# Sums over keys by 32 by 32 block transposes and row sums on VectorE, in place of products with ones

## The chip, the cores and the metric

The kernel runs on one core of one Trainium2 chip. The metric is the device time of one execution, in microseconds, as the median of a few runs. A profiled execution gives, beside its time, the span of the core's work and a record of every instruction. The engines go by the names of the profile: PE is TensorE's matrix products and PEld its weight loads, DVE is VectorE, ACT is ScalarE, SP is the engine that issues all DMAs here.

## What is computed

Two layers run over a batch of 32 items with 512 rows of 512 numbers each. The change concerns the first layer, attention with 8 heads, weighted by an adjacency matrix:

```python
logits = jnp.einsum('bhqd,bhkd->bhqk', q, k) / np.sqrt(DK)
logits = logits + jnp.log(jnp.clip(adj, ADJ_MIN, None))[:, None, :, :]
attn = jax.nn.softmax(logits, axis=-1)
out = jnp.einsum('bhqk,bhkd->bhqd', attn, v)
...
return _layer_norm(x + out @ Wo.T + bo, gamma, beta)
```

The kernel forms exp(q k / 8) * max(adj, 1e-8) without a maximum taken off, multiplies by v, and divides afterwards by the sum over the keys. That sum is what the change computes in another way. The second layer is a graph attention with one logit per row and column; it is touched only where the order of its steps moves.

## The kernel before

**Layout.** Items are pipelined over three stages: while item b goes through its attention, item b-1 gets its output product, layer norm and the logits of layer 2, and item b-2 gets the products of layer 2. Steady items (b = 2 to 30 of 32) run as two functions, `first_two(b)` for heads 0 to 3 and `second_two(b)` for heads 4 to 7; two heads are a "pair" p, so `first_two` has pairs 0 and 1. Items 0 and 1 run through `slot`, item 31 through `joining_slot`, `slot` and `last_slot`. The order of the instructions on PE, DVE, ACT and SP is written out by hand: each engine takes its own in program order, and the only freedom is in waiting.

**Scores.** `score(b, p, kc, halved)` (L842) multiplies 128 keys with all 512 queries for both heads of a pair. The result goes to PSUM, either a two-bank tile of `ps_s` (two such tiles in turn, shared with the tiles `f` of `seven_qk`) or two of the three `lone` banks. ACT takes the exponential into a tile `at` of 128 keys by (2 heads, 512 queries); eight `at` tiles turn. `factor` (L887) multiplies by the adjacency on DVE.

**Sums over keys before.** `sums_in_place` (L900) adds the four `at` tiles of a pair on DVE, three additions of 128 by 1024. That leaves a sum over 128 partitions. `divide(b, p)` (L924) does it for two pairs at once on PE: four products with ones, each of 32 columns, into `lone[0]`. ACT copies the bank to R (L936), and two DMAs take the 4 by 512 sums to memory and back as a tile `c` of 128 by 16 (L939, L941). `divided(b, p)` (L944) checks their range, inverts them on DVE, stores them to memory and loads them spread out into R (L956, L959). `scale(b, p)` (L968) multiplies the attention output oT of the two pairs by R on DVE.

**Where these stand.** In `first_two(b)`: `divide(last, 2)`, eight scores, the layer-2 product `seven_z(b-2)` with its additions `extra[...]` and the block transposes of eP between, `both` (products of `at` with v), `sums_in_place` of pairs 0 and 1, `seven_wo` (output product of item b-1, with DVE additions L774 and L778 that free its banks), `seven_qk` of pairs 2 and 3. In `second_two(b)`: `divide(b, 0)`, eight scores, `seven_out(b-2)` (additions L795 and L801), `both`, `seven_qk` and `seven_v` of the next item, `divided(b, 0)`, `scale(b, 0)`. L670 to L672 are the three additions with which DVE ends a `seven_qk` and frees its `f` tiles for the next scores.

**SP's queue.** In this order: eP copies of item b-1, `divide(last, 2)`'s two, `divided(last, 2)`'s three, the loads of n and x, `divide(b, 0)`'s two, the loads of the next adjacency, `divided(b, 0)`'s three, the eP copies of the next item.

Of the kernel before, what the change touches and what calls it, by code (L numbers as in the profile page):

```python
# [9 lines left out]
FP = mybir.dt.float32  # L10
I32 = mybir.dt.int32
AF = mybir.ActivationFunctionType
ALU = mybir.AluOpType
AX = mybir.AxisListType
# [5 lines left out]
P = 128  # L20
# [5 lines left out]
BL = 32  # L26
# [4 lines left out]
def kernel(  # L31
# [55 lines left out]
    nc = tc.nc  # L87
    B, N, D = x.shape
    DK = D // HEADS
    NC = N // P  # L90
# [376 lines left out]
    def scaled(s, cs):  # L467
        nc.vector.tensor_mul(s["yb"][:, cs, :], s["n"][:, cs, :], over(K["gamma"], cs))
# [39 lines left out]
    def fast(ctx):  # L508
# [6 lines left out]
        dram = ctx.enter_context(tc.tile_pool(name="dram", bufs=2, space=bass.MemoryType.DRAM))  # L515

        S = [dict() for _ in range(B)]
        lone = [ps_l.tile([P, N], FP, name=f"m{i}") for i in "xyz"]

        class Turns:  # L520
# [363 lines left out]
        def factor(b, p, kc):  # L884

            at = S[b]["at", p, kc]
            nc.vector.scalar_tensor_tensor(  # L887
                at, cT[:, kc, :].unsqueeze(1).to_broadcast([P, 2, N]), ADJ_MIN, at,
                ALU.max, ALU.mult,
            )  # L890
# [4 lines left out]
        def sums_in_place(b, p):  # L895

            s = S[b]
            to = s["as", p] = s["at", p, 0]
            return [
                lambda kc=kc: nc.vector.tensor_add(to, to, s["at", p, kc]) for kc in range(1, NC)  # L900
            ]

        def values(b, p):
            s = S[b]
            s.setdefault("oT", [None] * NPAIR)

            def part(half):
                if half == 0:
                    s["po", p] = ps_o.tile([P, N], FP, tag="po", name=f"po_{b}_{p}")
                for kc in (2 * half, 2 * half + 1):  # L910
                    for j in range(2):
                        h = 2 * p + j
                        nc.tensor.matmul(  # L913
                            s["po", p][j * DK : (j + 1) * DK, :],
                            s["v"][h // 4][:, kc, ts(h % 4, DK)],
                            s["at", p, kc][:, j, :],
                            start=(kc == 0), stop=(kc == NC - 1),
                        )
                if half == 1:
                    s["oT"][p] = act.tile([P, N], FP, tag="oT", name=f"oT_{b}_{p}", bufs=6)  # L920
                    nc.scalar.copy(s["oT"][p], s["po", p])  # L921
            return [lambda: part(0), lambda: part(1)]

        def divide(b, p):  # L924


            s = S[b]
            ps = lone[0]
            for h in range(4):
                nc.tensor.matmul(  # L930
                    ps[h * BL : (h + 1) * BL, :], ones[:, :BL], s["as", p + h // 2][:, h % 2, :],
                    start=True, stop=True,
                )
            s["R", p] = act.tile([P, 2, N], FP, tag="R", name=f"R_{b}_{p}")
            r = s["R", p][:, 0, :]
            nc.scalar.copy(r, ps)  # L936
            m = 4 * N // P
            d0 = dram.tile([4, N], FP, tag="d0", name=f"d0_{b}_{p}")
            nc.sync.dma_start(out=d0, in_=r.rearrange("(h r) n -> h r n", r=BL)[:, 0, :])  # L939
            c = small.tile([P, 2, m], FP, tag="c", name=f"c_{b}_{p}")  # L940
            nc.sync.dma_start(out=c[:, 0, :], in_=d0.rearrange("h (a m) -> (h a) m", m=m))  # L941
            s["c", p] = c

        def divided(b, p):  # L944
            s = S[b]
            c = s["c", p]
            m = 4 * N // P
            i = 2 * b + p // 2
            nc.vector.tensor_scalar(c[:, 1, :], c[:, 0, :], SUM_MAX, None, ALU.is_le)
            nc.vector.scalar_tensor_tensor(  # L950
                c[:, 1, :], c[:, 0, :], SUM_MIN, c[:, 1, :], ALU.is_ge, ALU.mult,
                accum_out=seen[:, i : i + 1],
            )
            nc.vector.reciprocal(c[:, 0, :], c[:, 0, :])
            d1 = dram.tile([P, m], FP, tag="d1", name=f"d1_{b}_{p}")
            nc.sync.dma_start(out=d1, in_=c[:, 0, :])  # L956
            d1 = d1.rearrange("(k j a) m -> j k (a m)", k=2, j=2)
            for j in range(2):
                nc.sync.dma_start(  # L959
                    out=s["R", p][j * DK : (j + 1) * DK, :, :],  # L960
                    in_=d1[j].unsqueeze(0).to_broadcast([DK, 2, N]),
                )

        def scale(b, p):
            s = S[b]
            for k in range(2):
                oT = s["oT"][p + k]
                nc.vector.tensor_mul(oT, oT, s["R", p][:, k, :])  # L968

        def first_difference(b, to=None):  # L970

# [51 lines left out]
        def seven_z(b):  # L1023


            s = S[b]
            n, e = s["n"], s["eP"]
            s["zT"] = zT = L1
            s1 = third
            t1 = S[b + 1]["R", 2][:, 1, :].rearrange("p (c n) -> p c n", c=KH)  # L1030
            A = {f"{i + 1}{j + 1}": n[:, ts(j, KH), ts(i, H)] for i in range(2) for j in range(2)}
            E = {f"{i + 1}{j + 1}": e[:, ts(j, KH), ts(i, H)] for i in range(2) for j in range(2)}
            C = {f"{i + 1}{j + 1}": zT[:, ts(i, KH), ts(j, H)] for i in range(2) for j in range(2)}
            left = {1: A["11"], 2: A["12"], 3: A["12"], 4: A["22"], 5: s1, 6: A["11"], 7: A["21"]}
            right = {1: E["11"], 2: E["21"], 3: E["22"], 4: E["21"], 5: t1, 6: E["11"], 7: E["12"]}
            ps = {}
            sub = nc.vector.tensor_sub

            def mul(i, name, first=False):
                for m in range(KH):  # L1040
                    for t in range(KH):
                        halves(
                            ps[name][:, m, :].rearrange("p (c n) -> p c n", c=KH),
                            left[i][:, t, ts(m, P)], right[i][:, :, ts(t, P)],
                            first and m == 0 and t == 0, m == KH - 1 and t == KH - 1,
                        )

            def unit0():
                ps.update(zip("bac", long_banks(f"z{b}")()))
                mul(1, "a", True)  # L1050
                mul(5, "c", True)
                nc.scalar.copy(ps["b"], ps["a"])
                nc.scalar.copy(C["22"], ps["c"])

            def unit1():
                mul(6, "a")
                mul(2, "b")
                nc.scalar.copy(C["12"], ps["a"])
                nc.scalar.copy(C["11"], ps["b"])

            def unit2():
                mul(7, "a")
                mul(3, "c")

            def unit3():
                mul(4, "a")
                nc.scalar.copy(C["21"], ps["a"])

            def before0():
                nc.vector.tensor_add(s1, A["21"], A["22"])  # L1070

            def before1():
                sub(t1, E["12"], E["11"])
                sub(A["21"], A["11"], A["21"])

            def after0():
                sub(E["11"], E["22"], t1)
                sub(A["11"], s1, A["11"])

            def after1():  # L1080
                sub(E["12"], E["22"], E["12"])

            def before2():
                sub(A["12"], A["12"], A["11"])
                sub(E["21"], E["21"], E["11"])

            def after2():
                nc.vector.tensor_add(C["22"], ps["a"], C["22"])

            def after3():  # L1090
                nc.vector.tensor_add(C["12"], ps["c"], C["12"])
            return [unit0, unit1, unit2, unit3], [
                before0, before1, after0, after1, before2, after2, after3
            ]

# [200 lines left out]
        def run(units):  # L1296
            for u in units:
                u()
# [181 lines left out]
        def first_two(b):  # L1480
# [12 lines left out]
            zs, extra = seven_z(b - 2)  # L1493
            extra[0]()
            factor(b, 0, 0)
            factor(b, 0, 1)
            run(eT(b - 2))
            extra[1]()
            zs[0]()
            extra[2]()  # L1500
            extra[3]()
            scaled(S[b - 2], slice(KH, NC))
            turn_a((2, 3))
            zs[1]()
# [18 lines left out]
            next_qk = seven_qk(b, 2)  # L1523
            next_qk[0]()
            both(b, 1)
            run(sums_in_place(b, 0))
            scale(last, 2)
            first_sum(last)
            run(next_qk[1:4])
            run(sums_in_place(b, 1))  # L1530
            run(next_qk[4:])
            next_qk = seven_qk(b, 3)
            wos[1]()
# [3 lines left out]
            wo_adds[1][0]()  # L1537
            offset_rows(S[b - 2], slice(KH, NC))
            run(wo_adds[1][1:])
            wos[3]()  # L1540
            run(wo_adds[2])
            next_qk[0]()
            wos[4]()
            run(wo_adds[3])
# [38 lines left out]
        def second_two(b):  # L1583
# [1 line left out]


            last, nxt = b - 1, b + 1
            divide(b, 0)
            eight_scores(b, (2, 3))
            z_sums(b - 2)  # L1590
            ks, qs = dots_units(S[last], small, S[b]["R", 0][:, 1, :], last)
# [324 lines left out]
```

## Time and profile before

| what | value |
|---|---|
| median of three runs | 3345.13 us (3344.17 to 3346.44) |
| the profiled execution | 3345.6 us, of which the span is 3343.8 us |
| one steady item | 102.8 us |
| products with ones, L930 | 464 records, 605 ns each; four run side by side |
| ACT's copy of the sums, L936 | 63, 585 to 588 ns each |
| scaling with R, L968 | 126, 684 ns each |
| block transposes of 512 columns, L576 and L598 | 678 to 688 ns each |
| additions of 1024 columns, L900 | 348, 1218 ns each |

Instructions of DVE overlap a little at their ends, so a row of equal ones takes less than the sum of its durations: four transposes of 512 columns take 2.49 us. A matrix product in fp32 shows as two passes, and two products that fill different parts of the array show side by side; the duration of one says little, and the chain of waits says what a group of them costs. The TensorE clock was 1.0 in the whole run.

### The profile page before, as it was taken

The page shows a single profiled execution, that of the slowest core. Times are in us where ns is not written, and L with a number is a line of the kernel's source. Part 1 is how long each engine was busy: PE and PEld are TensorE (multiplying, and loading weights), DVE is VectorE, ACT ScalarE, POOL GpSimd, SP SyncE. Part 2 cuts the span into 40 slices and gives each one's busy share as a digit, 9 for nine tenths or more (in the row PEclk, how much of TensorE's full clock was granted, in tenths as well). Part 3 has the DMA queues.
Part 4 walks back from the last instruction along what each step waited for, and adds up shares of the span by engine and source line. Part 5 has one row for each costly group of instructions (what it writes and reads, how often), then busy time and mean ns, then how long its engine had stood idle before and what let it go on. Part 6 is the DMA issues. An engine that isn't in the chain of part 4 may idle for free.

```text
span 3343.8 us, 64256 instructions
## 1 busy us (share of the span) xinstructions
PE 3326.2 (99%) x25914; PEld 1929.8 (58%) x25914; DVE 3001.7 (90%) x5313; ACT 1407.5 (42%) x2559; POOL 0.9 (0%) x9
## 2 busy tenths in 40 slices
PE   9999999999999999999999999999999999999999
PEld 4555555565555555565555655556565656555545
DVE  7889898899988999889989889898899888998988
ACT  3444433434444344334443443444434434444343
POOL 0000000000000000000000000000000000000000
PEclk9999999999999999999999999999999999999999
DMA  5234242343433433334424234343343333442321
GB/s 127 45 75 93 61 85 66 68 93 67 87 69 60 89 83 71 74 58 86 93 61 85 62 71 93 67 87 69 58 92 83 71 74 58 86 93 61 84 71 48
DMA packets 881655, 252.84 MB, mean 76 GB/s; under 512 B 806732, under 2 KB 809036, under 8 KB 881352
## 3 DMA queue, kind: packets, MB, share of 16 engines
q1 hardware_dynamic: 881352, 248.67, 36.2%
q8 instruction: 206, 3.38, 0.4%
q14 instruction: 97, 0.79, 0.1%
HBM read 182.46 MB, written 34.65 MB: 65 GB/s over the span
## 4 chain that ended last, share of the span: by engine, by line
PE 97%; DVE 2%; ACT 1%; DMA 0%; issue 0%; SPq 0%; DVEq 0%; ACTq 0%
PE f L213 22%; PE mx L213 15%; PE my L213 15%; PE mz L213 15%; PE po L913 13%; PE sc L852 8%; PE my L852 2%; PE mx L852 2%; PE mz L852 2%; PE mx L930 1%; PE my L930 1%; PE mz L930 1%; PE mz L490 0%; PE my L326 0%; DVE at L869 0%
## 5 line engine op out<-in xcount | busy, mean ns | idle before, releaser
L887 DVE SCALAR_TENSOR_TENSOR at<-cT,at 128x1024 f32<-128x1024 f32 x468 | 551.7, 1216 | 0.0
L913 PE MATMUL po<-at,v 128*64 128x512 f32 x2048 | 467.6, 594 | 2.0 <-DVE fold_more L298 1.6
L900 DVE TENSOR_TENSOR at<-at,at 128x1024 f32<-128x1024 f32 x348 | 423.9, 1218 | 8.0
L861 ACT ACTIVATE at<-sc 128x1024 f32<-128x1024 f32 x328 | 332.9, 1075 | 53.4 <-PE sc L852 53.4
L852 PE MATMUL sc<-qT,kT 64*128 64x512 f32 x1312 | 317.3, 593 | 0.4 <-ACT at L861 0.4
L913 PEld LDWEIGHTS po<-at,v 128*64 128x64 f32 x2048 | 146.4, 137 | 247.4 <-issue 160.9
L921 ACT COPY oT<-po 128x512 f32<-128x512 f32 x128 | 74.9, 585 | 480.7 <-PE po L913 480.7
L213 PE MATMUL f<-xT,wq 128*64 128x256 f32 x2032 | 263.3, 379 | 0.0
L213 PE MATMUL f<-T,qk_s 128*64 128x256 f32 x2032 | 252.3, 379 | 0.1
L852 PEld LDWEIGHTS sc<-qT,kT 64*128 64x128 f32 x1312 | 120.2, 186 | 165.7 <-ACT at L861 79.8
L213 PEld LDWEIGHTS f<-xT,wq 128*64 128x64 f32 x2032 | 149.5, 137 | 97.1 <-issue 35.6
L213 PEld LDWEIGHTS f<-T,qk_s 128*64 128x64 f32 x2032 | 149.4, 137 | 82.6 <-issue 16.1
L655 ACT COPY f<-f 128x256 f32<-128x256 f32 x127 | 45.3, 357 | 345.4 <-PE f L213 345.4
L661 ACT ACTIVATE qT<-f,bq 128x256 f32<-128x256 f32 x127 | 60.1, 473 | 217.8 <-PE f L213 217.8
L852 PE MATMUL my<-qT,kT 64*128 64x512 f32 x254 | 133.5, 605 | 0.0
L213 PE MATMUL f<-xT,wk 128*64 128x256 f32 x1016 | 131.6, 379 | 0.0
L213 PE MATMUL f<-T,wk 128*64 128x256 f32 x1016 | 131.6, 379 | 0.0
L213 PE MATMUL f<-xT,qk_s 128*64 128x256 f32 x1016 | 131.6, 379 | 0.0
L852 PE MATMUL mz<-qT,kT 64*128 64x512 f32 x248 | 130.5, 606 | 0.0
L852 PE MATMUL mx<-qT,kT 64*128 64x512 f32 x234 | 123.2, 606 | 0.0
L213 PE MATMUL my<-eP,n 128*64 128x256 f32 x960 | 114.9, 380 | 2.2 <-DVE eP L576 1.7
L213 PE MATMUL mx<-eP,n 128*64 128x256 f32 x960 | 114.6, 380 | 0.5 <-DVE eP L576 0.5
(430 smaller groups left out, 6275.9 us busy)
## 6 DMA issues: line engine op xcount, KB each, us to landing
cT<-in_adj_dram SPq DMA_DIRECT2D x512, 64.0 KB
R<-d SPq DMA_DIRECT2D x126, 256.0 KB
x<-in_x_dram SPq DMA_DIRECT2D x124, 256.0 KB
n<-in_x_dram SPq DMA_DIRECT2D x31, 1024.0 KB
L<-in_adj_dram SPq DMA_DIRECT2D x60, 512.0 KB
eP<-L SPq DMA_DIRECT2D x480, 64.0 KB
out_dram<-yb SPq DMA_DIRECT2D x58, 512.0 KB
w<-dk SPq DMA_DIRECT2D x32, 256.0 KB
```

What stands on the lines that cost most here:

```text
L213: nc.tensor.matmul(to[ts(h, DK)], left[:, ts(h, DK)], right, start=start, stop=stop, skip_group_check=True,)
L655: nc.scalar.copy(ps["b"], ps["a"])
L661: nc.scalar.activation(q[:, H:], ps["a"], AF.Identity, bias=bq)
L852: nc.tensor.matmul(parts[j], s["kT", p][rows, ts(kc, P)], s["qT", p][rows, :], start=True, stop=True,)
L861: nc.scalar.activation(at, sc, AF.Exp, scale=SCALE)
L887: nc.vector.scalar_tensor_tensor(at, cT[:, kc, :].unsqueeze(1).to_broadcast([P, 2, N]), ADJ_MIN, at, ALU.max, ALU.mult,)
L900: lambda kc=kc: nc.vector.tensor_add(to, to, s["at", p, kc]) for kc in range(1, NC)
L913: nc.tensor.matmul(s["po", p][j * DK : (j + 1) * DK, :], s["v"][h // 4][:, kc, ts(h % 4, DK)], s["at", p, kc][:, j, :], start=(kc == 0), s ...
L921: nc.scalar.copy(s["oT"][p], s["po", p])
L930: nc.tensor.matmul(ps[h * BL : (h + 1) * BL, :], ones[:, :BL], s["as", p + h // 2][:, h % 2, :], start=True, stop=True,)
```

## The change

For pairs 0 and 1 of the steady items (`folded`, b = 2 to 30) the products with ones, ACT's copy and its two DMAs go. In their place `folded_sums(b)` returns, for each pair, the three additions of before (into the last `at` tile instead of the first) and two further DVE steps: the summed tile is transposed in place in blocks of 32 by 32, and a row sum over 32 elements reduces 128 by 1024 to 128 by 32. This adds 32 keys at a time, so four parts are left, one for each group of 32 partitions. `move_sums(b)` writes the 128 by 64 result to memory and reads it back with four DMAs in pieces of 16 numbers, so that the four parts of one query stand in one partition; `divided(b, 0)` adds them with one more small reduction. The inverted sums then stand in R in another order of queries (query 32 m + q at place 16 q + m), and `scale` reads R with a step of 16 numbers.

In the hand-written order the transposes and row sums stand in `first_two` between the groups of additions of `seven_wo`, with `move_sums` behind them. `second_two` only sets up the tile R where it called `divide(b, 0)`. Two other steps move: `A["21"]`'s subtraction goes from `before1` to `before0` of `seven_z`, ahead of the eP transposes (also in `joining_slot`, which shares it), and `factor(b, 0, 1)` goes from ahead of the eP transposes to behind `extra[3]`.

```diff
+        folded = {(b, 0) for b in range(2, B - 1)}
...
+        def folded_sums(b):
+            s = S[b]
+            s["ks"] = ks = small.tile([P, 4, 16], FP, tag="ks", name=f"ks_{b}", bufs=2)
+
+            def of(p):
+                to = s["at", p, NC - 1]
+                flat = to.rearrange("p j n -> p (j n)")
+                return [
+                    lambda kc=kc: nc.vector.tensor_add(to, to, s["at", p, kc])
+                    for kc in range(NC - 1)
+                ], [
+                    lambda: nc.vector.transpose(flat, flat),
+                    lambda: nc.vector.tensor_reduce(
+                        ks[:, 2 * p : 2 * p + 2, :].rearrange("p h m -> p (h m)"),
+                        flat.rearrange("p (a k) -> p a k", k=BL), AX.X, ALU.add,
+                    ),
+                ]
+            return of(0), of(1)
+
+        def move_sums(b):
+            s = S[b]
+            d0 = dram.tile([P, 64], FP, tag="d0", name=f"d0_{b}_0")
+            nc.sync.dma_start(out=d0, in_=s["ks"].rearrange("p h m -> p (h m)"))
+            c = small.tile([P, 4, 16], FP, tag="c4", name=f"c4_{b}", bufs=1)
+            for h in range(4):
+                nc.sync.dma_start(
+                    out=c[h * BL : (h + 1) * BL],
+                    in_=d0[:, h * 16 : (h + 1) * 16].rearrange("(k q) m -> q k m", q=BL),
+                )
+            s["c4"] = c
...
         def divided(b, p):
...
+            if (b, p) in folded:
+                c = small.tile([P, 2, m], FP, tag="c", name=f"c_{b}_{p}", bufs=2)
+                nc.vector.tensor_reduce(
+                    c[:, 0, :], s["c4"].rearrange("p k m -> p m k"), AX.X, ALU.add
+                )
+            else:
+                c = s["c", p]
...
         def scale(b, p):
             s = S[b]
             for k in range(2):
-                oT = s["oT"][p + k]
-                nc.vector.tensor_mul(oT, oT, s["R", p][:, k, :])
+                oT, r = s["oT"][p + k], s["R", p][:, k, :]
+                if (b, p) in folded:
+                    oT = oT.rearrange("p (m q) -> p m q", q=BL)
+                    r = r.rearrange("p (q m) -> p m q", q=BL)
+                nc.vector.tensor_mul(oT, oT, r)
...
             def before0():
                 nc.vector.tensor_add(s1, A["21"], A["22"])
+                sub(A["21"], A["11"], A["21"])
 
             def before1():
                 sub(t1, E["12"], E["11"])
-                sub(A["21"], A["11"], A["21"])
...
         def first_two(b):
...
             factor(b, 0, 0)
-            factor(b, 0, 1)
             run(eT(b - 2))
...
             extra[3]()
+            factor(b, 0, 1)
             scaled(S[b - 2], slice(KH, NC))
...
-            run(sums_in_place(b, 0))
+            sum0, sum1 = folded_sums(b)
+            run(sum0[0])
...
-            run(sums_in_place(b, 1))
+            run(sum1[0])
...
             run(wo_adds[1][1:])
+            run(sum0[1])
             wos[3]()
             run(wo_adds[2])
+            run(sum1[1])
+            move_sums(b)
...
         def second_two(b):
...
-            divide(b, 0)
+            S[b]["R", 0] = act.tile([P, 2, N], FP, tag="R", name=f"R_{b}_0")
```

More of the change, by code (lines that the diff above doesn't have):

```diff
@@ L939, in divide @@
             nc.sync.dma_start(out=d0, in_=r.rearrange("(h r) n -> h r n", r=BL)[:, 0, :])
-            c = small.tile([P, 2, m], FP, tag="c", name=f"c_{b}_{p}")
+            c = small.tile([P, 2, m], FP, tag="c", name=f"c_{b}_{p}", bufs=2)
             nc.sync.dma_start(out=c[:, 0, :], in_=d0.rearrange("h (a m) -> (h a) m", m=m))
@@ L945, in divided @@
             s = S[b]
-            c = s["c", p]
             m = 4 * N // P
             i = 2 * b + p // 2
+            if (b, p) in folded:
+                c = small.tile([P, 2, m], FP, tag="c", name=f"c_{b}_{p}", bufs=2)
+                nc.vector.tensor_reduce(
[3 more added lines that the diff above has]
+                c = s["c", p]
             nc.vector.tensor_scalar(c[:, 1, :], c[:, 0, :], SUM_MAX, None, ALU.is_le)
```

## The prediction

> **What bounds the kernel now.** I read the page first, then the chain of waits, then the busy time by stage over two halves of one steady item, and last the timelines of VectorE and TensorE around the two places that the change touches. The page and its chain:
>
> ```profile
> PE 3326.2 (99%) x25914; PEld 1929.8 (58%) x25914; DVE 3001.7 (90%) x5313; ACT 1407.5 (42%) x2559; POOL 0.9 (0%) x9
> ...
> PE 97%; DVE 2%; ACT 1%; DMA 0%; issue 0%; SPq 0%; DVEq 0%; ACTq 0%
> ```
>
> TensorE sets the time, and VectorE has 10% left. So a TensorE microsecond taken off is worth one only while VectorE is not late. By stage, from the start of one `divide` to the next:
>
> ```profile
> 1738.30:1789.66 51.36, 51.36 (x413) 29.55 (x416) 45.25 (x72) 18.26 (x32) 0.00 (x0) 1.00 0.35 61
> 1789.66:1841.13 51.47, 51.47 (x413) 29.49 (x416) 48.20 (x95) 25.58 (x48) 0.00 (x0) 1.00 0.39 88
> ```
>
> The columns are the stretch, its length, and the busy time of PE, PEld, DVE, ACT, POOL, then clock, DMA share and GB/s. VectorE is idle 6.11 us in the first half (`first_two`) but only 3.27 us in the second (`second_two`). What `divide(b, 0)` costs on the chain (start, us, what):
>
> ```profile
> 1785.35 4.32 PE f L213 x40
> 1789.66 1.00 PE mx L930 x8
> 1790.66 0.62 PE my L852
> ```
>
> Its four products run side by side: 1.00 us an item, not 4 x 0.6.
>
> Where VectorE waits before that point (start, us, instruction, idle before it):
>
> ```profile
> 1778.56 0.69 DVE L778 TENSOR_TENSOR n<-mx,n 128x512 f32<-128x512 f32 x1 [0.18 <-PE mx L213]
> 1779.16 0.68 DVE L778 TENSOR_TENSOR n<-mz,n 128x512 f32<-128x512 f32 x1
> 1780.21 0.69 DVE L778 TENSOR_TENSOR n<-my,n 128x512 f32<-128x512 f32 x1 [0.37 <-PE my L213]
> 1781.94 0.69 DVE L778 TENSOR_TENSOR n<-mx,n 128x512 f32<-128x512 f32 x1 [1.04 <-PE mx L213]
> 1785.39 0.69 DVE L778 TENSOR_TENSOR n<-mx,n 128x512 f32<-128x512 f32 x1 [2.76 <-PE mx L213]
> ...
> 1790.05 0.41 DVE L672 TENSOR_TENSOR kT<-f,kT 128x256 f32<-128x256 f32 x1
> ```
>
> Idle of 0.37 + 1.04 + 2.76 us is the cover for the new work. After it VectorE is packed until L672, and L672 frees the bank of the second score of `second_two`.
>
> The other place is the start of `first_two`:
>
> ```profile
> 1736.57 1.28 DVE L968 TENSOR_TENSOR oT<-oT,R 128x512 f32<-128x512 f32 x2
> ...
> 1737.77 1.30 DVE L598 STREAM_TRANSPOSE cT<-cT 128x512 f32<-128x512 f32 x2
> ...
> 1739.63 0.41 DVE L672 TENSOR_TENSOR kT<-f,kT 128x256 f32<-128x256 f32 x1
> ...
> 1740.19 1.88 PE L852 MATMUL sc<-qT,kT 64*128 64x512 f32 x8
> ```
>
> `scale(b, 0)` is the L968 pair. L672 ends at 1740.04 and the score that needs its bank starts at 1740.19. A handoff from VectorE to a waiting TensorE costs as much:
>
> ```profile
> 1438.65 0.69 DVE L1073 TENSOR_TENSOR R<-eP 128x512 f32<-128x512 f32 x1
> ...
> 1439.49 1.95 PE L213 MATMUL my<-R,third 128*64 128x256 f32 x16
> ```
>
> 1438.65 + 0.69 = 1439.34, so 0.15 us. At 1740 there is therefore no slack (0.03 us at most): whatever VectorE is late by in `second_two`, TensorE pays.
>
> **What the Trainium skill says.** "SBUF — State Buffer", section "Door 1: The DMA port swizzle", gives SBUF lines of 16 bytes, full rate only with two or more hits on a line, and a penalty where each access goes to a new one; "GPSIMD Engine Reference", section "Performance pitfalls for Q7 kernels", measures one cycle more an element (1.9 to 2.9) for steps over 8 bytes on GpSimd. No VectorE row of this trace has such a step with enough elements to show it. "VectorE: DVE Perf Modes", section "The perf-mode tier table", has `tensor_reduce` at one element a cycle; the trace has no large one. The same page, section "Walkthrough: the 8-slice pipeline in each mode", says of the plain 1x mode that it "makes no assumptions. fp32, weird strides, PSUM operands — all work"; the trace agrees on the rate for dense fp32 (1024 elements in 1.14 us), and is silent on steps.
>
> **Part by part, per item, for the 29 items b = 2 to 30.**
>
> Removed: four products, 1.00 us of TensorE; the first score pass costs 0.62 us after it against 0.42 for the next, and I leave that 0.2 where it is, since `slot` shows it after products of 64 columns too (1.92 against 1.72 for the first score at 119.85). ACT's copy (0.585 us) and two small DMAs are off the path.
>
> Added in `first_two`: two in-place transposes and two row sums, of 1024 elements a partition. The transpose is taken from L576: 2.49 us for four of 512, as fast as a tensor_tensor, so 1.14 for 1024 like L887 (4.62 for four):
>
> ```profile
> 1758.70 4.62 DVE L887 SCALAR_TENSOR_TENSOR at<-cT,at 128x1024 f32<-128x1024 f32 x4
> ...
> 1763.90 3.74 DVE L900 TENSOR_TENSOR at<-at,at 128x1024 f32<-128x1024 f32 x3
> ```
>
> L900, each reading its forerunner's output, steps by (3.74 - 1.22)/2 = 1.26. So a pair is 1.26 + 1.14 = 2.40, two are 4.80. Bounds for a row sum: 1.07 (1024 elements at the rate of L887's step) to twice 1.14.
>
> Placed from 1779.76: first pair to 1782.16, two L778 to 1783.36 (the second ends 1783.45; TensorE's last product of `seven_wo` wants its bank at 1783.45 in stream, stall about 0.12), second pair to 1785.76, against 1785.39 before. So L672 ends 0.37 later, 1790.83, and the second score starts 1790.98 (0.15 handoff). TensorE alone would be there at 1791.55 - 1.00 + 0.12 = 1790.67. VectorE ends last, and of 1.00 us only 1791.55 - 1790.98 = 0.57 is gained. The wait at L795 (1.72 idle before it) takes up 0.57 + 0.37, so nothing is carried from there into the rest of `second_two`.
>
> Added in `second_two`: the reduction over four parts, 64 elements to 16, about 0.24 (L949's 0.17, its 0.21 step to a dependent, a few more elements). Then `scale(b, 0)`: L968 now reads R at steps of 64 bytes. Bounds: no extra (step 0.60 each) and one cycle more an element, 512 / 0.96 GHz = 0.53 us each, 1.07 for both. Nothing excludes either; a gain is excluded. I take 1.07, since two pages price it and none says that VectorE is exempt. Behind it on VectorE stand L598, L670 and L672, and the second score waits for L672: 0.24 + 1.07 - 0.03 = 1.28 us of TensorE stall.
>
> Moved: L1074 ahead of the eP transposes (in `joining_slot` it leaves a chain that TensorE waits for: about 0.6 us once), and one L887 to behind L1081. The latter stands before L1084, which has 0.93 idle before it: 1.14 - 0.93 - cadence 0.09 leaves it 0.12 late, L1088 also, and the product that waits for L1088's bank about 0.10.
>
> Moved on SP: the small store and four gathers of 64-byte pieces are issued near 1786, after the loads of x (issued until 1772) and before anything at 1804; the result is needed at 1829.8. Some 6 us for five DMAs (the old pair took 1.7 us from issue to next issue) leave over 30 us. Without that cover each late microsecond would be one of VectorE's, then TensorE's. The d1 store, the R loads and the eP copies behind them on SP come 0.24 later, but TensorE is 1.28 later too.
>
> Sum: -0.57 + 1.28 + 0.10 = +0.81 us, times 29 = +23.5. Eight items lost 3.4 us to late eP copies (halves of 51.5 to 52.3 instead of 51.36); with TensorE later, most of that goes: -3.4. Joining item: -0.6. Together +19.5: the profiled execution's 3345.6 (span 3343.8 plus 1.8) becomes 3365; the median shown, 3345.13, lies 0.5 under it, so 3364.5. 3364.
>
> **The rivals.**
> (a) The strided read is free. Then +0.24 - 0.03 + 0.10 - 0.57 = -0.26, times 29 = -7.5, joining -0.6: 3337, faster. For it: the sentence on weird strides. Deciding point: 0.26 us for both multiplications, 0.13 each.
> (b) A part penalty, about a third more (0.2 each): +0.14 an item, 3348, no change.
> (c) Row sums at two cycles an element: 1.07 more for each of two, all of it at the second score: 2.14 x 29 = +62 on the forecast, 3426. Against it: the one-cycle price of the page.
> (d) VectorE is nowhere late: the whole 1.00, 29 us, 3316. Against it: the packed stretch to L672.
> (e) The gathers land late: needs 30 us more; under 1%.
>
> **How the numbers follow.** Forecast 0.58, (a) 0.28, (b) 0.08, (c) 0.03, (d) 0.03. About 0.2% (6.7 us) is what a measurement can tell from no change. Faster: most of (a), and (d): 0.26. Same: a part of (a), (b), a little of the forecast: 0.14. Slower: 0.60. The forecast's own range is 3355 to 3374 (row sums 0.15 longer each add 9). Signs are split, so the range takes (a) in: 3334 to 3374.
>
> **What would show it.** Right: L968 of pair 0 at 1.1 to 1.2 us instead of 0.68, L672 ending over 1 us later against `divide`, TensorE idle over 1 us before the second score of `first_two`, transposes of 1024 and row sums of 1.2 us each. Wrong: L968 unchanged (then a), or TensorE waiting before the second score of `second_two` for longer than 0.4 us (then c). No cover in the gathers would show as VectorE idle before its 64-element sum.

## The result, and the profile after

The changed kernel takes 3327.82 us (median of 6 runs, 3326.12 to 3329.62), the kernel before 3344.56 in the same comparison. The ratio is 0.9949, with an interval of 0.9936 to 0.9962. It is faster by 16.7 us, 0.5%. The forecast was 3364 us, slower by 19, with a range of 3334 to 3374: wrong in sign, and the time lies under the range.

The page of the changed kernel's profiled execution (3328.74 us, span 3327.0), busy times and the shares of the chain that ended last:

```profile
PE 3307.9 (99%) x25682; PEld 1892.2 (57%) x25682; DVE 3153.7 (95%) x5458; ACT 1393.4 (42%) x2530; POOL 0.9 (0%) x9
...
PE 65%; DVE 24%; DMA 5%; ACT 3%; issue 2%; SPq 2%; DVEq 0%; ACTq 0%
```

VectorE is busy 152 us longer and stands at 95%; TensorE is busy 18 us less. The chain now runs over VectorE for 24%. That number says little: a chain goes to whatever released an instruction last, even where the release cost nothing. TensorE is still busy 99% of the span, so what counts is where TensorE starts late.

The same two halves of a steady item in the changed kernel (columns as in the prediction; the cut between them is now the first score of `second_two`, since the product that marked it is gone):

```profile
1728.02:1779.79 51.77, 51.72 (x411) 29.40 (x409) 50.32 (x77) 18.36 (x32) 0.00 (x0) 1.00 0.34 62
1779.79:1830.25 50.46, 50.46 (x403) 29.26 (x401) 48.27 (x96) 24.99 (x47) 0.00 (x0) 1.00 0.40 90
```

Between the same points of the kernel before (its products start at 1738.23, the first score of `second_two` at 1790.59):

```profile
1738.23:1790.59 52.36, 52.36 (x419) 29.71 (x417) 46.25 (x75) 18.26 (x32) 0.00 (x0) 1.00 0.34 60
1790.59:1841.06 50.47, 50.47 (x404) 29.32 (x400) 47.20 (x92) 25.58 (x48) 0.00 (x0) 1.00 0.40 89
```

So the second half is unchanged, and the first gives 0.59 us: 1.00 of products removed, less 0.41 lost again. Times 29 items, 0.59 is 17.1 us; the spans differ by 16.8.

The new and the slower instructions, from the costliest groups of the changed kernel (line, engine, operation, tiles, count, then busy us, mean ns and idle before; L1013 is `scale`, L917 the transpose, L918 the row sum, L986 the sum of the four parts):

```profile
L1013 DVE TENSOR_TENSOR oT<-oT,R 128x512 f32<-128x512 f32 x126 | 100.7, 841 | 0.0
L917 DVE STREAM_TRANSPOSE at<-at 128x1024 f32<-128x1024 f32 x58 | 71.6, 1235 | 0.0
L918 DVE TENSOR_REDUCE ks<-at 128x32 f32<-128x1024 f32 x58 | 70.8, 1221 | 2.0
L986 DVE TENSOR_REDUCE c<-c 128x16 f32<-128x64 f32 x29 | 7.4, 254 | 0.0
```

L1013 mixes 68 dense and 58 strided ones; 841 ns is no instruction's duration. With 684 for the dense ones (L968 before), the strided ones are (126 x 0.841 - 68 x 0.684) / 58 = 1.03 us each. (The busy time of the group, 100.7, is less than 126 x 0.841, because neighbours overlap.)

**Where 0.32 of the 0.41 is lost: the start of `first_two`.** First the kernel before, its timeline there (start, us, instruction, idle before it; the rows of a view count passes up to its end, and four passes are one score; L930 is `divide(last, 2)`, L670 the first of the three additions; the last one, L672, ended at 1740.04):

```profile
1738.23 1.07 PE L930 MATMUL mx<-at,ones 128*32 128x512 f32 x8
1738.99 0.39 DVE L670 TENSOR_TENSOR qT<-f,qT 128x256 f32<-128x256 f32 x1
...
1739.76 0.19 PEld L852 LDWEIGHTS sc<-qT,kT 64*128 64x128 f32 x2 [0.23 <-issue]
...
1740.19 1.02 PE L852 MATMUL sc<-qT,kT 64*128 64x512 f32 x4
```

The weights of the second score load at 1739.76, before L672 ends. In the places below where this score does wait, its weights load only after the release (1730.19, 1846.21), so this speaks against a wait for L672, though the score starts 0.15 after its end; the experiments settle it. By them, L670 was the one that the score needed, and that was done at 1739.38. This line was there to be read before the prediction. Now the same place in the changed kernel (the same lines of the program stand one to 45 further down: L671 and L673 are the first and the last addition, L966 the products, L853 the score):

```profile
1726.65 1.97 DVE L1013 TENSOR_TENSOR oT<-oT,R 128x512 f32<-128x512 f32 x2
1728.02 1.06 PE L966 MATMUL mx<-at,ones 128*32 128x512 f32 x8
1728.54 1.29 DVE L599 STREAM_TRANSPOSE cT<-cT 128x512 f32<-128x512 f32 x2
1729.76 0.38 DVE L671 TENSOR_TENSOR qT<-f,qT 128x256 f32<-128x256 f32 x1
1730.19 0.30 PEld L853 LDWEIGHTS sc<-qT,kT 64*128 64x128 f32 x4 [0.88 <-DVE qT L671]
1730.20 1.13 PE L853 MATMUL sc<-qT,kT 64*128 64x512 f32 x4
1730.40 0.40 DVE L673 TENSOR_TENSOR kT<-f,kT 128x256 f32<-128x256 f32 x1
```

The weight load waits for L671, the first addition, and the score starts 0.06 after that ends, while the last addition, L673, runs until 1730.80. Counted from the products, the first addition ends at 1.15 us before (1739.38 - 1738.23) and at 2.12 after: 0.97 later, 0.69 of it the two strided multiplications (1.97 against 1.28 us), the rest the reduction. The score starts at 1.96 before and 2.18 after: 0.22 later. So the kernel before had 0.75 us of slack here, where the prediction had 0.03. The score then takes 0.10 more: its weights were not loaded ahead, and its first pass takes 0.53 us to the next one instead of 0.43. The fourth score starts at 1732.02, 4.00 us after the products, against 3.68 before. Together 0.32.

**The other end: `second_two`.** The packed stretch of VectorE before it, and the second score there (timeline of the changed kernel; L779 are `seven_wo`'s additions):

```profile
1769.85 1.24 DVE L917 STREAM_TRANSPOSE at<-at 128x1024 f32<-128x1024 f32 x1
...
1771.12 1.22 DVE L918 TENSOR_REDUCE ks<-at 128x32 f32<-128x1024 f32 x1
...
1772.26 0.68 DVE L779 TENSOR_TENSOR n<-my,n 128x512 f32<-128x512 f32 x1
...
1772.85 0.68 DVE L779 TENSOR_TENSOR n<-mx,n 128x512 f32<-128x512 f32 x1
...
1773.59 1.49 PEld L213 LDWEIGHTS mx<-wo_s,oT 128*64 128x64 f32 x16 [0.34 <-DVE n L779]
...
1779.72 0.39 DVE L671 TENSOR_TENSOR qT<-f,qT 128x256 f32<-128x256 f32 x1
...
1780.36 0.42 DVE L673 TENSOR_TENSOR kT<-f,kT 128x256 f32<-128x256 f32 x1
...
1780.75 1.45 PE L853 MATMUL sc<-qT,kT 64*128 64x512 f32 x6
```

The second score starts at 1780.75, before L673 ends at 1780.78, so it cannot have waited for it, and L671 had been done for 0.64 us. TensorE starts that score 0.96 after the first one at 1779.79, the same distance as in `first_two` before (1739.23 to 1740.19): no wait. The whole 1.00 us of the products is kept here, not 0.57. The remaining 0.10 of the loss is the weight load at 1773.59, which waits for an addition behind the first transpose and row sum, as forecast.

### The profile page after: what moved, and what is told of

Its sections match the earlier page's. It is cut to its first block, busy times and chain, and to the rows that moved or that the text cites. A ratio compares the mean times of both kernels' runs of the same rounds, so it can differ in the third digit from the quotient of the medians.

```text
span 3327.0 us, 64024 instructions
## 1 busy us (share of the span) xinstructions
PE 3307.9 (99%) x25682; PEld 1892.2 (57%) x25682; DVE 3153.7 (95%) x5458; ACT 1393.4 (42%) x2530; POOL 0.9 (0%) x9
## 4 chain that ended last, share of the span: by engine, by line
PE 65%; DVE 24%; DMA 5%; ACT 3%; issue 2%; SPq 2%; DVEq 0%; ACTq 0%
PE f L213 14%; PE mx L213 10%; PE mz L213 10%; PE my L213 10%; PE sc L853 8%; PE po L949 8%; DVE at L888 5%; DVE yb L802 4%; DVE R L392 3%; DMA out_dram<-yb 2%; DVE L L436 2%; DMA eP<-L 2%; DVE L L446 2%; ACT L L451 2%; PE my L853 2%
## 5 line engine op out<-in xcount | busy, mean ns | idle before, releaser
L853 PE MATMUL sc<-qT,kT 64*128 64x512 f32 x1312 | 319.8, 597 | 2.4 <-DVE qT L671 0.7
L853 PEld LDWEIGHTS sc<-qT,kT 64*128 64x128 f32 x1312 | 120.8, 185 | 174.4 <-ACT at L862 71.0
L853 PE MATMUL my<-qT,kT 64*128 64x512 f32 x254 | 133.5, 605 | 0.0
L853 PE MATMUL mz<-qT,kT 64*128 64x512 f32 x248 | 130.5, 606 | 0.0
L853 PE MATMUL mx<-qT,kT 64*128 64x512 f32 x234 | 123.2, 606 | 0.0
```

The source lines that it names most:

```text
L853: nc.tensor.matmul(parts[j], s["kT", p][rows, ts(kc, P)], s["qT", p][rows, :], start=True, stop=True,)
```

## The experiments

The question was which addition frees the second score's bank. Theory F: the first one, so the second score has slack and the removed products pay in full. Theory L, the prediction's own reading: the last one, with no slack. A third, M: the moved steps carry the gain. The kernel before took 3344.46 us (median) in the runs shared by the first four experiments and 3344.78 in those of the others.

**R read without a step.** The changed kernel, with `scale` reading R densely. The divisors then meet other queries, so the output is another one; the instructions are the same in number and size.

```diff
                 if (b, p) in folded:
-                    oT = oT.rearrange("p (m q) -> p m q", q=BL)
-                    r = r.rearrange("p (q m) -> p m q", q=BL)
+                    r = r
```

> The changed kernel, but scale reads R of pair 0 without a step, so the sums meet the wrong queries. Theory F (first addition): the bank of the second score of first_two is freed by the first addition of seven_qk (L671), which had about 0.7 us to spare in the kernel before and is 0.98 us late in the changed one; the stepped read is 0.69 us of that. Without it the lateness is 0.29 us, the stall of about 0.26 us an item goes, 29 x 0.26 = 7.5 us: near 3320 us. Theory L (last addition, no slack, as the prediction had it): every bit of lateness is paid, 0.69 x 29 = 20 us: near 3308 us. Theory M (the gain comes from the two moved steps): no change from 3328 us.

3319.59 us, ratio 0.9922 (0.9909 to 0.9936). That is 8.2 us under the changed kernel, as F has it; an item takes 101.92 us instead of 102.23, and 0.31 is the whole loss at the second score. Had the penalty been paid in full, it would have been 0.69 x 29 = 20 us.

**The transposes behind the additions.** The changed kernel, with the two transposes that stand between `scale` and the additions put behind them:

```diff
             scale(b, 0)
-            turn_a((0, 1))
             run(seven_qk(nxt, 1))
+            turn_a((0, 1))
```

> The changed kernel with the two transposes of turn_a((0, 1)) behind seven_qk(nxt, 1) in second_two, so that its three additions come 1.2 us earlier on VectorE. Theory F: the stall of 0.26 us an item before the second score of first_two goes, near 3320 us. Theory L: 0.98 us an item, 28 us, near 3300 us. Theory M: no change from 3328 us.

3319.87 us, ratio 0.9926 (0.9912 to 0.9939): F again. All work is still there. The additions come 1.2 us earlier, and again 0.31 us an item is gained and no more. Its timeline there (L966 are the products):

```profile
1724.90 1.07 PE L966 MATMUL mx<-at,ones 128*32 128x512 f32 x8
1725.41 0.43 DVE L671 TENSOR_TENSOR qT<-f,qT 128x256 f32<-128x256 f32 x1
...
1726.41 1.30 DVE L599 STREAM_TRANSPOSE cT<-cT 128x512 f32<-128x512 f32 x2
...
1726.86 1.88 PE L853 MATMUL sc<-qT,kT 64*128 64x512 f32 x8
```

The second score stands 1.96 us behind the products, as in the kernel before.

**A delay ahead of all three additions.** The kernel before, with three small additions on VectorE:

```diff
+        pad = const.tile([P, P], FP, name="pad")
+        nc.gpsimd.memset(pad, 1.0)
...
             turn_a((0, 1))
+            for _ in range(3):
+                nc.vector.tensor_add(pad, ones, ones)
             run(seven_qk(nxt, 1))
```

> The kernel before with three VectorE additions of 128 by 128 (0.2 us each, 0.6 us in all) ahead of seven_qk(nxt, 1) in second_two. Theory F: within the 0.7 us of slack, 0 to +3 us (3344.6 to 3348). Theory L: 0.57 us an item, +16.5 us, near 3361 us.

3351.36 us, ratio 1.0022 (1.0014 to 1.0029): 6.9 us slower, between the two. The dose was larger than thought:

```profile
1844.16 1.06 PE L932 MATMUL mz<-at,ones 128*32 128x512 f32 x8
1844.92 0.90 DVE L1650 TENSOR_TENSOR pad<-ones 128x128 f32<-128x128 f32 x3
...
1845.74 0.42 DVE L672 TENSOR_TENSOR qT<-f,qT 128x256 f32<-128x256 f32 x1
...
1846.21 0.30 PEld L854 LDWEIGHTS sc<-qT,kT 64*128 64x128 f32 x4 [0.76 <-DVE qT L672]
1846.22 1.99 PE L854 MATMUL sc<-qT,kT 64*128 64x512 f32 x8
```

The first addition (L672 in this kernel) ends 2.00 us after the products, 0.85 later than before. With the slack of 0.75 read above, the score should start 0.10 late. It does: 2.06 against 1.96. With another 0.10 for the weights not loaded ahead, 0.20 x 29 = 5.8 of the 6.9 us. L, at this dose, would have cost (0.85 - 0.03) x 29 = 24 us for the wait alone. So the run decides against L, but only with its trace: both forecasts, 0 to 3 us and 16.5 us, missed, since they were worked out from too small a dose.

**The same delay between the first addition and the other two.** The kernel before, where only theory L has the second score late:

```diff
...
-        def seven_qk(b, p):
+        def seven_qk(b, p, late=False):
...
                 nc.vector.tensor_add(q[:, H:], ps["c"], q[:, H:])
+                if late:
+                    for _ in range(3):
+                        nc.vector.tensor_add(pad, ones, ones)
                 nc.vector.tensor_add(k[:, H:], ps["a"], k[:, H:])
...
-            run(seven_qk(nxt, 1))
+            run(seven_qk(nxt, 1, True))
```

> The kernel before with the same 0.6 us of VectorE work between the first addition (q) and the two others (k) of that seven_qk. Theory F: the first addition is not moved and the third score's bank has 0.9 us to spare, 0 to +3 us. Theory L: the last addition is what counts, +16.5 us, near 3361 us.

3352.92 us, ratio 1.0023 (1.0014 to 1.0033). It is 8.5 us slower, and again both forecasts missed. The time alone does not separate the theories; the timeline does (L672 is the first addition here, L677 the last):

```profile
1845.57 1.06 PE L935 MATMUL mz<-at,ones 128*32 128x512 f32 x8
...
1846.34 0.38 DVE L672 TENSOR_TENSOR qT<-f,qT 128x256 f32<-128x256 f32 x1
...
1847.53 1.99 PE L857 MATMUL sc<-qT,kT 64*128 64x512 f32 x8
...
1847.82 0.41 DVE L677 TENSOR_TENSOR kT<-f,kT 128x256 f32<-128x256 f32 x1
...
1848.35 0.33 PEld L857 LDWEIGHTS sc<-qT,kT 64*128 64x128 f32 x4 [0.63 <-PE my L857]
```

The second score starts 1.96 us after the products, unmoved, 0.70 us before the last addition ends at 1848.23. This excludes L directly. The row of 8 passes holds two scores; the weights of the third load at 1848.35, just behind that end, and it is the third score that loses here: 0.07 us by the start of the next. So the two `ps_s` tiles come free one by one, the second score's by the first addition, the third's by the last. The other 0.15 us an item comes further down, most of it in `seven_z`, where TensorE's products start up to 0.17 later than before. What in it is late was not taken apart. The halves show 0.22 an item, 6.4 of the 8.5 us; some 2 more are single items that took longer than the others (5.3 us in all in this execution, 3.3 before). The prediction puts such items down to late eP copies; no run here tests that.

**The moved steps put back.** The changed kernel, with `A["21"]` and `factor(b, 0, 1)` where they stood before:

```diff
             factor(b, 0, 0)
+            factor(b, 0, 1)
             run(eT(b - 2))
...
             extra[3]()
-            factor(b, 0, 1)
             scaled(S[b - 2], slice(KH, NC))
...
             def before0():
                 nc.vector.tensor_add(s1, A["21"], A["22"])
-                sub(A["21"], A["11"], A["21"])
...
             def before1():
                 sub(t1, E["12"], E["11"])
+                sub(A["21"], A["11"], A["21"])
```

> The changed kernel with the two moved steps (A["21"] and factor(b, 0, 1)) put back where they were. Theory M: they carry the gain, near 3344 us. Theory F: the gain is the removed products' 1.00 us less the stalls; without the moves the eP transposes start 0.54 us later against the scores, which the 0.45 us to spare before the second product of seven_z doesn't cover, and the third product gets its operands some 0.3 us late: 0.1 to 0.35 us an item, 3331 to 3338 us.

3328.46 us, ratio 0.995 (0.9937 to 0.9964), the changed kernel's time within 0.6 us. M falls. What F had added for the moves, 0.1 to 0.35 us an item, was too much as well: they cost and bring nothing that can be measured.

**Transposes and row sums taken out.** In their place a copy of 32 columns for each pair, so that the last part of the sums over keys, over the 128 partitions, is left out:

```diff
-                    lambda: nc.vector.transpose(flat, flat),
-                    lambda: nc.vector.tensor_reduce(
+                    lambda: nc.vector.tensor_copy(
                         ks[:, 2 * p : 2 * p + 2, :].rearrange("p h m -> p (h m)"),
-                        flat.rearrange("p (a k) -> p a k", k=BL), AX.X, ALU.add,
+                        flat[:, :BL],
                     ),
```

> The changed kernel with the transposes and row sums left out: 32 columns of each summed tile are copied into ks instead, so the divisors are other numbers. Theory F: the two pairs stand in idle time of VectorE but for 0.10 us an item at the last product of seven_wo: 2.9 us, near 3325 us. The prediction's reading, in which they cost 0.43 us of the gain at the second score of second_two: 12.5 us, near 3315 us.

3323.96 us, ratio 0.9937 (0.9924 to 0.9951). Some 4.8 us of VectorE work an item is worth 3.9 us in all, 0.13 an item (the usual item takes 102.11 us instead of 102.23): the 0.10 at `seven_wo` and little else. Had the second score of `second_two` waited for VectorE, as the prediction had it, 0.43 an item would have come back.

**Both losses mended.** The changed kernel with the transposes behind the additions, and with both row sums behind the additions `wo_adds[2]` of `seven_wo`, for which its last product waits:

```diff
             run(wo_adds[1][1:])
-            run(sum0[1])
+            run(sum0[1][:1])
             wos[3]()
             run(wo_adds[2])
-            run(sum1[1])
+            run(sum1[1][:1])
+            run(sum0[1][1:])
+            run(sum1[1][1:])
             move_sums(b)
...
             scale(b, 0)
+            run(seven_qk(nxt, 1))
             turn_a((0, 1))
-            run(seven_qk(nxt, 1))
```

> The changed kernel with turn_a((0, 1)) behind seven_qk(nxt, 1), and the order of the new steps in first_two as transpose 0, wo_adds[2], transpose 1, sum 0, sum 1. Theory F: both stalls go (0.26 and 0.10 us an item): 3317 us, 3 us under the run with the late turn_a alone. If the second stall isn't that of the last product of seven_wo: 3320 us.

3316.55 us, ratio 0.9914 (0.99 to 0.9927), faster than both kernels, and 3.3 us under the run with the late transposes alone: 0.11 an item, the loss at `seven_wo`. Its first half:

```profile
1722.78:1774.14 51.36, 51.36 (x410) 29.48 (x408) 49.92 (x74) 18.27 (x32) 0.00 (x0) 1.00 0.36 63
```

51.36 is 52.36 - 1.00: the products' whole microsecond, with VectorE still at 49.92 of 51.36. 28.2 us under the kernel before is 0.97 x 29.

**What a step costs.** One execution of the changed kernel with multiplications of 128 by 512 put ahead of its work, the second operand read with a step of 1, 2, 4, 8 and 16 numbers, then the first operand, both, and the result with 16, and last the second operand with 32:

```diff
...
+        for _ in range(2):
+            nc.vector.tensor_mul(pad_o, pad, pad)
+            nc.vector.tensor_mul(pad_o.rearrange("p (m q) -> p m q", m=2), pad.rearrange("p (m q) -> p m q", m=2), pad.rearrange("p (q m) -> p m q", m=2))
...
```

> The changed kernel with products of 128 by 512 on VectorE added at its start, the second operand read with steps of 1, 2, 4, 8, 16 and 32 numbers, then the first operand, both operands and the result with a step of 16. From the changed kernel's L1013 (1.03 us against 0.68): step 16 near 1.03. If lines of 16 bytes count, step 2 as step 1, steps 4 to 32 alike, slower than step 1. If only both streams together count, a stepped first operand costs as the second, and both more.

The timeline of VectorE there, in that order:

```profile
3.28 0.69 DVE L1796 TENSOR_TENSOR L<-L 128x512 f32<-128x512 f32 x1 [3.28 <-POOL L L1793]
4.01 0.69 DVE L1797 TENSOR_TENSOR L<-L 128x512 f32<-128x512 f32 x1
4.74 1.07 DVE L1798 TENSOR_TENSOR L<-L 128x512 f32<-128x512 f32 x1
5.84 1.09 DVE L1799 TENSOR_TENSOR L<-L 128x512 f32<-128x512 f32 x1
6.97 1.04 DVE L1800 TENSOR_TENSOR L<-L 128x512 f32<-128x512 f32 x1
8.04 1.03 DVE L1801 TENSOR_TENSOR L<-L 128x512 f32<-128x512 f32 x1
9.11 1.03 DVE L1802 TENSOR_TENSOR L<-L 128x512 f32<-128x512 f32 x1
10.17 1.02 DVE L1803 TENSOR_TENSOR L<-L 128x512 f32<-128x512 f32 x1
11.22 1.03 DVE L1804 TENSOR_TENSOR L<-L 128x512 f32<-128x512 f32 x1
```

A step of 2 numbers (8 bytes) is free; from 4 numbers (16 bytes) on, it costs 0.33 to 0.40 us for 512 elements, about half the dense time. With a step of 16, it is the same on whichever operand, and two strided operands cost no more than one. The second round of the same nine took the same times within 0.02 us.

## Why the prediction was wrong, point by point

- **"L672 frees the bank of the second score", "VectorE ends last", "only 1791.55 - 1790.98 = 0.57 is gained".** This step failed: the wait for L672. The first addition frees that bank, the last one the third score's. At `second_two` VectorE was not last: 1.00 us was gained, and the second score started before the last addition ended. The delay between the additions showed the same directly at the start of `first_two`.
- **"At 1740 there is therefore no slack (0.03 us at most)."** The same error a second time, and the larger: 0.75 us of slack. An instruction that starts 0.15 us after another ends was taken for one that waits for it, because a real handoff elsewhere took as long. The distance was a coincidence, and the weight load at 1739.76 spoke against a wait; at that real handoff (1439.34 to 1439.49) the weights load at 1439.46, after the release. So the stall of 1.28 us was 0.32.
- **The strided read, 1.07 for two.** A term mis-sized: 0.69. The one more cycle an element that the Trainium skill has for GpSimd ("GPSIMD Engine Reference", section "Performance pitfalls for Q7 kernels") was carried over as 0.53 us for 512; VectorE took 0.35. That "two pages price it" is too much: only this one has a figure, the other names a penalty without one. With the reduction, lateness was 0.97 instead of 1.31. At this size alone, without slack, the sum would still have been -0.57 + 0.97 - 0.03 + 0.10 = +0.47 an item, slower; so the slack decided the sign. With both waits read rightly but 1.07 for the read, the stall would have been 1.31 - 0.75 = 0.56 and some 0.10 for the weights: -1.00 + 0.66 + 0.10 = -0.24, faster.
- **The reduction of four parts, 0.24.** It follows as 0.97 - 0.69 = 0.28, and the changed kernel's timeline has 0.29 from its start (1818.95) to the next instruction (1819.24); 0.04 too little.
- **A pair of transpose and row sum, 2.40.** Measured 1772.26 - 1769.85 = 2.41. **The stall in `seven_wo`, 0.12**: 0.10. **The gathers hidden**: they were used some 40 us after their issue (1778.54 to 1818.95), and VectorE has no wait before L986.
- **The moved `factor`, +0.10, and joining, -0.6.** Putting both moves back changed the time by 0.6 us, within what the runs spread. Neither is shown.
- **Late eP copies, -3.4.** Counted as what single items take above the usual one (where it is more than 0.1 us), they cost 2.5 us in the profiled execution of the changed kernel and 4.2 in that of the best version, against 3.3 before: nothing reliable, and no term of the sum should have stood on it.
- **Two readings that changed nothing.** The lower bound of 1.07 for a row sum is not "the rate of L887's step", which is (4.62 - 1.22) / 3 = 1.13. The 0.2 that the first score costs more is the chain's way of counting: by the starts of its passes (1790.59, 1791.12, 1791.55) it is 0.10.
- **The signs named.** Transposes and row sums of 1.2 us came, L672 ending 0.97 us later against the products nearly so. The sign that failed is TensorE idle over 1 us before the second score of `first_two`: the score was 0.22 late. Neither of the two signs of being wrong came, for neither asked whether the wait was there at all.
- **The rivals.** (a), a free strided read, named the direction for a reason that is wrong. (d), "VectorE is nowhere late", given 0.03, was the nearest in mechanism: at 3316 it is what the best version reached (3316.55), and the change itself stands 0.41 us an item short of it.

The corrected sum: -1.00 + 0.32 + 0.10 = -0.58 an item, times 29 = -16.8 us. The spans gave -16.8 and the medians -16.7. That this fits to 0.1 us is partly luck: single items alone differ by about 1 us between the two executions.

## What to carry to other kernels

When an instruction starts just behind another, ask for proof that it waits: the weight load ahead of the product, the buffer it writes, and that buffer's last reader. Instructions that free two buffers can free them one at a time, as here, and each buffer then has its own slack. An engine that is busy 95% need not cost anything where what the bound engine waits for stands first in its order: here moving two transposes behind three additions, and two row sums behind others, took the gain from 16.7 to 28.2 us without removing any work.

## What the runs showed of the hardware

- **Strided fp32 on VectorE.** A multiplication of 128 by 512 takes 0.69 us with a step of 8 bytes, as when dense, and 1.02 to 1.09 with 16 bytes and more. The Trainium skill, "SBUF — State Buffer", section "Door 1: The DMA port swizzle", asks for two hits or more on each line of 16 bytes; the runs agree on both sides of that. Its remark that one can stride 4 fp32 for free does not hold here: a step of 4 cost 0.38. "GPSIMD Engine Reference", section "Performance pitfalls for Q7 kernels", has half as much again an element for steps over 8 bytes on GpSimd. The edge is the same here, and the whole instruction grew by 1.03 / 0.69 = 1.49. That is no rule for other sizes: 512 more dense elements take 1.218 - 0.684 = 0.53 us in the kernel before, so if the rest is a fixed part, the elements alone went from 0.53 to 0.88, by some 1.6 times (an estimate; only 512 elements were run).
- **Row sums.** "VectorE: DVE Perf Modes", section "Rules for kernel authors", calls `tensor_reduce` the slowest operation of VectorE. In fp32 it is not: 1.221 us for 128 by 1024 against 1.224 for an addition of that size and 1.235 for the block transpose.
- **A product whose weights come late** costs more than its wait: in the second score 0.10 us beyond the 0.22.
- **Small instructions.** Three additions of 128 by 128 into one tile step by 0.27 us each (0.82 for three, 1844.92 to 1845.74), where the expectation had reckoned with 0.2 each.
